# Loading and rounding down_w a second time, across the turn from the first batch to the second, in a one-core GLU kernel

## The chip, the core and the metric

The kernel runs on one core of one Trainium2 chip. The metric is the device time of one launch in microseconds (us), and the times shown are medians over runs on the chip. Engines are called PE (TensorE), DVE (VectorE), ACT (ScalarE), POOL (GpSimd) and SP (SyncE, which issues nearly all DMAs). Every engine works through its own instructions in the order in which they were written, and an instruction that has to wait for another engine or for a DMA holds up everything behind it on its engine.

## What is computed

Four batches of 1024 tokens with 512 features go through a gated block. Cut to what matters, the reference is:

```python
scale = cond @ norm_w.T + 1.0
h = x * (scale[:, None, :] * rsqrt(mean(x * x) + 1e-6))
val, gate = split(h @ up_w.T, 2)             # 2 x 2048 columns
h = val * gelu(gate)
hq = act_quant(h)                            # per token: round(h * 127 / max|h|), and back
wq = weight_quant(down_w)                    # round(down_w / mean|down_w|) cut to -1, 0, 1, and back
y = hq @ wq.T + x
```

weight_quant needs the mean of |down_w| over the whole matrix before any element can be rounded. down_w is 512 x 2048 in float32, 4 MB.

## The kernel before, in words

**Batches and slots.** The four batches run one after another, and each has 16 slots, one for every 128 columns of val and of gate. The text counts slots through the whole kernel: g = 0 to 15 is the first batch, g = 16 to 31 the second, and so on. All products of up_w are made with float16 pairs (a high and a low part).

In the first batch a slot is two calls of plain_half (L623), one for each half of 512 tokens, with 12 matmuls into a bank pg (gate), a Gelu on ACT (L629), 12 matmuls into a bank pv and a multiplication on DVE (L633). Meanwhile up_w is loaded, scaled and summed into the seven weight tiles of a Strassen product, and these sums are spilled to DRAM (s_dram, s_spill L398). The tokens of the second batch are normalized and transposed in slots 6 to 13 (class Tokens, L493).

From the second batch on a slot is one call of slot (L658) with seven products of six matmuls each, called here p0 to p6 after the number that the code gives them (L580 to L586). In the steady state PE runs p0, p4, p1 of slot g, p3 of slot g - 1, p5 of g, p2 of g - 1, p6 of g. Slot 16 has no predecessor and runs p0, p4, p5, p1, p6. p1 adds onto a bank B that ACT first fills with a copy of A after p0 (L675), p5 goes on in A after that copy, and p6 goes on in A once ACT has copied A after p5 (L668). So three short ACT copies stand between products of PE in every slot.

**Loads of the sums.** A slot's weights are loaded back from s_dram into one of two buffers SXY, in four DMAs on SP: s_load_x (L420) brings the two tiles of p0 and p1 as they are (L418, 256 KB, called part one here) and those of p4, p5 and p6 through a transposing DMA (L416, 384 KB, part two); s_load_y (L424) brings those of p2 and p3. Those of slot g + 2 are issued in slot g, each as soon as PE has read what stood in its buffer. Issuing is itself work on SP and shows in the timeline: some 0.3 to 0.6 us for a plain DMA, 1.2 us or more for a transposing one.

**down_w.** Its eight parts of 128 x 1024 (d_load, L442, 512 KB each) are loaded near the start into the half R[:, 1] of a large buffer and summed by ACT (d_sum, L446) in slots 1 to 3. Slot 4 makes the mean (d_mean, L455). From slot 5 to slot 12 ACT rounds each part where it stands (d_round, L461, an Activation of 128 x 1024) and writes its sign as float8 into a tile tn (d_put, L468, a second Activation); after every second part SP transposes tn into wd (L475), four times in all. D_ROUND (L1073) says which part in which slot. wd is read from slot 25 on, by d_sums and then by the down products.

**Order of the work.** All of it is written out by hand for the first batch (first_batch, L1093). In the later batches slot() calls back at three places x, y and z, and two lists (class Filler, L1258) hand work to DVE and to ACT there: items have a first place, a cost in us and in some cases a last place, and run in order as far as a budget goes. The list act holds the rounding of the batch before from slot 19 on. loads() (L1431) issues the s_loads at the end of a slot.

Of the kernel before, what the change touches and what calls it, by code (L numbers as in the profile page):

```python
# [9 lines left out]
F32 = mybir.dt.float32  # L10
F16 = mybir.dt.float16
BF16 = mybir.dt.bfloat16
F8 = mybir.dt.float8e4
I32 = mybir.dt.int32
AF = mybir.ActivationFunctionType
# [4 lines left out]
P = 128  # L20
EXPONENT = 0x7F800000
MAGIC = 1.5 * 2.0**23
# [29 lines left out]
def glu_quant_kernel(  # L52
# [360 lines left out]
    def s_load(g, c0, c1, turn=False):  # L413
        s, d = s_tile(g)[:, c0:c1], s_dram[g % NJ, :, c0 * 2 * HALF : c1 * 2 * HALF]
        if turn:
            SP.dma_start_transpose(s.rearrange("p c w (k f) -> p (c w k) f", k=2), d)  # L416
        else:
            SP.dma_start(out=s.rearrange("p c w f -> p (c w f)"), in_=d)  # L418

    def s_load_x(g):  # L420
        s_load(g, Y_TO, C_ALL)
        s_load(g, 0, Y_FROM, True)

    def s_load_y(g):  # L424
        s_load(g, Y_FROM + 1, Y_TO)
        s_load(g, Y_FROM, Y_FROM + 1, True)
# [8 lines left out]
    def d_part(n):  # L435
        return R[:, 1, n * HF : (n + 1) * HF]

    def d_at(n):

        return n // 4 + 2 * (n % 2), n // 2 % 2, n % 2  # L440
# [14 lines left out]
    def d_mean(part):  # L455
# [2 lines left out]
        DVE.tensor_scalar(wmean, pm, 1.0 / (D * FF), 1e-5, ALU.mult, ALU.max)  # L458
        DVE.reciprocal(wsc, wmean)

    def d_round(n):  # L461

        dn = d_part(n)
        ACT.activation(dn, dn, AF.Copy, scale=wsc, bias=MAGIC)

    tn = []

    def d_put(n):  # L468
        _, u, y = d_at(n)
        if y == 0:  # L470
            tn.append(wpool.tile([P, HF], BF16, name=f"tn_{n}", tag="v"))
        t8 = tn[-1].bitcast(F8).rearrange("p (f y) -> p f y", y=2)
        ACT.activation(t8[:, :, y], d_part(n), AF.Sign, bias=unmagic, saturate=False)
        if y:
            SP.dma_start_transpose(wd[:, n // 4, u], tn[-1])  # L475

    def w_block(name):
        k, y = W_AT[name]
# [144 lines left out]
    def plain_half(j, h, between=nothing):  # L623
        whole = j == WHOLE
        tag = ("po", 3) if whole else ("A", 2) if h or j == 1 else ("B", 1)
        pg = bank(*tag, name=f"pg_{j}_{h}")
        plain(j, 1, h, pg)
        t1 = wpool.tile([P, TOK], F32, name=f"g_{j}_{h}", tag="t1")
        ACT.activation(t1, pg, AF.Gelu, scale=gain(j, 1))  # L629
        between()  # L630
        pv = bank(*(("po", 3) if whole and not h else ("E", 2)), name=f"pv_{j}_{h}")
        plain(j, 0, h, pv)
        DVE.scalar_tensor_tensor(h_half(j, h), pv, gain(j, 0), t1, ALU.mult, ALU.mult)  # L633
# [436 lines left out]


    D_SUM = {0: (4, 5), 1: (6, 7), 2: (2, 3), 3: (0, 1)}
    D_ROUND = {5: (0, 1), 6: (2,), 7: (3,), 9: (4,), 10: (5,), 11: (6,), 12: (7,)}  # L1073
    D_MEAN = 4
    TOKENS = {6: 0, 8: 1, 10: 2, 12: 3}
    LARGEST = {
# [16 lines left out]
    def first_batch(j, sc):  # L1093

        if j + 2 <= LATE:
            w_load(j + 4)
        if j >= 4:
            next_tokens(j + 2)
        t = toks.get(j)
        odd = t is not None and j not in TOKENS  # L1100
        n = j + 2
        rows = LATE <= n < NJ
        if j + 1 < LATE:
            s_sums(j + 1)
        elif rows:
            s_sums(n)
        if j + 3 < NJ:
            w_range(j + 3)
            w_gain(j + 3)
        if j == D_MEAN:  # L1110
            part = d_total()
        plain_half(j, 0)
        for i, h in LARGEST.get(j, ()):
            for f in pair_max(0, i, h):
                f()
        if n < LATE:
            w_scale(n)
            w_rows(n)
        if j + 1 < LATE:
            s_all(j + 1)  # L1120
        if t and not odd:
            t.norm()
        for m in D_ROUND.get(j, ()):
            d_round(m)
            d_put(m)
        if t and not odd:
            t.scale(sc)
            t.sums()
        if j + 2 > LATE and j + 5 < NJ:
            w_load(j + 5)  # L1130
        if odd:
            t.high()
            t.low(DVE)
        if odd:
            t.turn()
        plain_half(j, 1)
        if j == 3:
            pd = cond_spread(dg, 1, B, "po")
            cond_undo(pd, 1, B)
            cond_rows()  # L1140
        if j == D_MEAN:
            d_mean(part)
        own = rows and j + 1 >= LATE

        def next_rows():
            if LATE <= j + 3 < NJ:
                w_scale(j + 3)
                w_rows(j + 3)

        if odd:  # L1150
            next_rows()
        if own:
            s_high(n)
            s_low(n, POOL)
        if not odd:
            next_rows()
        if own:
            s_spill(n)
        elif rows:
            s_sums(n)  # L1160
            s_all(n)
            w_load(j + 5)
        for n in D_SUM.get(j, ()):
            d_sum(n)
        if j in (NJ - 3, NJ - 1):
            s_load_x(NJ + (j - NJ + 3) // 2)
            s_load_y(NJ + (j - NJ + 3) // 2)


    def second_slot():  # L1170
# [163 lines left out]
    for b in range(1, B):  # L1334
        dve, act = Filler(), Filler()
        gains(b)
        am = am_tile(b - 1)
        dq = state[b - 1] = sm.tile([P, 2 * NA], F32, name=f"dq_{b}", tag="dq")
        last_pair = NJ // 2 - 1
        for h in range(2):  # L1340
            add_pair(
# [38 lines left out]
        for j in range(NJ):  # L1380
            g = b * NJ + j
            down = b + 1 < B and j in DOWN
            if down:
                pair, a = pairs[j], DOWN[j]
                xrs = [down_load(b - 1, h, a) for h in range(2)]
            early_sums, late_sums = D_SUM_AT.get((b, j), ((), ()))
            left = SLOT_US + PAIR_US * down - OWN_US + 0.4
            more = D_SUM_US * len(late_sums) + 0.7 * (j + 1 == min(DOWN) and b + 1 < B)
            left -= D_SUM_US * len(early_sums) + more
            mine = {p: [sum(c[e] for _, c in steps.get((j, p), ())) for e in range(2)] for p in "xyz"}  # L1390
            left -= sum(mine[p][0] for p in "xyz")
            act_left = {"x": 2.7, "y": 2.2 if down else 1.1, "z": 0}

            def run(p):
                nonlocal left
                for f, _ in steps.get((j, p), ()):
                    f()
                if p == "x":
                    cap = min(left, 3.9 - mine["x"][0] - (0 if down else mine["y"][0] + more))
                    left -= cap - dve.run((j, p), cap)  # L1400
                elif p == "z":
                    left = dve.run((j, p), left)
                if p != "z":
                    act.run((j, p), act_left[p] - mine[p][1])

            def early():
                if down:
                    pair.first([po_bank(f"po_{b}_{a}_{n}") for n in range(3)])
                    pair.sums(None, h_slots(g)[:, 0, 1])
                d_sums(early_sums)  # L1410

            def next_pair():
                if b + 1 < B and j + 1 in DOWN:
                    pairs[j + 1] = Pair(b - 1, DOWN[j + 1])
                    pairs[j + 1].sum1(h_slots(g + 1)[:, 0, 0])

            def more_sums():
                next_pair()
                d_sums(late_sums)

            mid = [nothing] * 3
            if j + 1 == min(DOWN):
                mid[0] = more_sums
            if down:
                mid = [
                    lambda: (next_pair(), pair.third(xrs, dq), d_sums(late_sums)),
                    pair.fourth,
                    lambda: (loads(), pair.fifth()),
                ]

            def loads():  # L1431
                if NJ + 2 <= g + 2 < B * NJ:
                    s_load_x(g + 2)
                if NJ + 2 <= g + 1 < B * NJ:
                    s_load_y(g + 1)


            if b + 1 == B and j in DOWN and DOWN[j] < 3:
                pairs[DOWN[j]] = Pair(b - 1, DOWN[j])
                places = old_places(DOWN[j])  # L1440
                pairs[DOWN[j]].sum1(places[0])
                pairs[DOWN[j]].sums(*places[1:])
            if j == 4:
                token_turn(b - 1, am)
            if j == 5:
                bring_dq = token_undo(b - 1, dq)
            if j == 6:
                bring_dq()
            if j == NJ - 1:
                get_ready()  # L1450
            elif b == 1 and j == 0:
                get_ready()
            slot(g, lambda: run("x"), lambda: run("y"), lambda: run("z"), early, mid)
            if not down:
                loads()
# [169 lines left out]
```

## Time and profile before

| what | value |
|---|---|
| time, median of 3 runs | 725.74 us (725.62 to 725.95) |
| span of the profiled execution | 724.0 us |
| granted TensorE clock | 1.000 |
| busy: PE, DVE, ACT, POOL | 716.5, 584.2, 397.6, 201.6 us |
| DMA moved | 117.85 MB, mean 163 GB/s |
| first batch's last matmuls (slot 15) end | about 184.2 us |

The span runs from the first to the last instruction of one profiled execution. The timed runs hold 1.7 us more, which lies around the span. A row of a timeline gives start, duration, engine, line, operation and tiles; several instructions in a row of one line are merged, with their count behind the x. In a row of windows each engine's busy time stands with its instruction count, then the granted clock (1.00 is full), the busy share of the DMA engines and the rate that they moved.

### The profile page before, as it was taken

The page shows a single profiled execution, that of the slowest core. Times are in us where ns is not written, and L with a number is a line of the kernel's source. Part 1 is how long each engine was busy: PE and PEld are TensorE (multiplying, and loading weights), DVE is VectorE, ACT ScalarE, POOL GpSimd, SP SyncE. Part 2 cuts the span into 40 slices and gives each one's busy share as a digit, 9 for nine tenths or more (in the row PEclk, how much of TensorE's full clock was granted, in tenths as well). Part 3 has the DMA queues.
Part 4 walks back from the last instruction along what each step waited for, and adds up shares of the span by engine and source line. Part 5 has one row for each costly group of instructions (what it writes and reads, how often), then busy time and mean ns, then how long its engine had stood idle before and what let it go on. Part 6 is the DMA issues. An engine that isn't in the chain of part 4 may idle for free.

```text
span 724.0 us, 10200 instructions
## 1 busy us (share of the span) xinstructions
PE 716.5 (99%) x3678; PEld 359.9 (50%) x3678; DVE 584.2 (81%) x824; ACT 397.6 (55%) x625; POOL 201.6 (28%) x207
## 2 busy tenths in 40 slices
PE   7999999999999999999999999999999999999998
PEld 3544444444444446655444445666444444445854
DVE  8977999984698899887689897687678888755896
ACT  6768868861337674554335676544433665333473
POOL 1579788882100034440000030360020000000120
PEclk9999999999999999999999999999999999999999
DMA  9579999996654564977846646766955455453253
GB/s 317 190 231 271 300 287 251 276 229 152 117 103 102 132 150 127 208 174 167 174 102 103 131 102 176 200 155 159 216 105 103 101 104 100 102 101 97 103 174 119
DMA packets 224191, 117.85 MB, mean 163 GB/s; under 512 B 186486, under 2 KB 196871, under 8 KB 224140
## 3 DMA queue, kind: packets, MB, share of 16 engines
q1 hardware_dynamic: 223850, 116.87, 66.1%
q8 instruction: 29, 0.48, 0.3%
q10 hardware_dynamic: 290, 0.33, 0.1%
q14 instruction: 22, 0.18, 0.1%
HBM read 49.50 MB, written 23.09 MB: 100 GB/s over the span
## 4 chain that ended last, share of the span: by engine, by line
PE 98%; DMA 1%; ACT 0%; SPq 0%; issue 0%; DVE 0%; ACTq 0%
PE A L586 34%; PE E L586 17%; PE pg L601 11%; PE pv L601 11%; PE po L880 9%; PE B L586 9%; PE po_end L832 4%; DMA H<-in_x_dram 1%; PE ptx L981 1%; PE pv L648 0%; PE po_B L880 0%; PE pg L648 0%; PE pw L339 0%; PE po_A L880 0%; PE po_E L880 0%; ACT R L947 0%
## 5 line engine op out<-in xcount | busy, mean ns | idle before, releaser
L586 PEld LDWEIGHTS <-SXY 128*128 128x128 f16 x2016 | 196.9, 98 | 231.3 <-issue 0.6
L586 PE MATMUL A<-R,SXY 128*128 128x512 f16 x1152 | 266.0, 379 | 0.0
L586 PE MATMUL E<-R,SXY 128*128 128x512 f16 x576 | 140.0, 379 | 0.1
L688 DVE SCALAR_TENSOR_TENSOR H<-A,sg,t 128x512 f32<-128x512 f32 x48 | 36.0, 750 | 67.9 <-PE A L586 67.7
L740 POOL PARTITION_ALL_REDUCE am<-R x8 | 14.3, 1793 | 234.0 <-DVE R L726 234.0
L804 DVE TENSOR_TENSOR H<-H,am 128x1024 f32<-128x1024 f32 x64 | 76.1, 1215 | 0.0
L601 PEld LDWEIGHTS <-SXY 128*128 128x128 f16 x486 | 47.4, 98 | 57.4 <-DVE SXY L372 0.5
L701 ACT ACTIVATE t<-t,sg 128x512 f32<-128x512 f32 x48 | 34.6, 721 | 67.8 <-DVE t L698 67.7
L586 PE MATMUL B<-R,SXY 128*128 128x512 f16 x288 | 70.0, 379 | 0.0
L724 DVE TENSOR_REDUCE gm<-H 128x512 f32<-128x1024 f32 x56 | 69.0, 1233 | 1.0
L601 PE MATMUL pg<-R,SXY 128*128 128x512 f16 x252 | 58.0, 379 | 0.0
L601 PE MATMUL pv<-R,SXY 128*128 128x512 f16 x234 | 54.4, 380 | 0.0
L685 ACT ACTIVATE t<-B,sg 128x512 f32<-128x512 f32 x48 | 33.0, 687 | 36.3 <-PE B L586 36.3
L880 PE MATMUL po<-wd,R 128*128 128x256 fp8e4 x416 | 52.5, 273 | 0.0
L490 POOL TENSOR_SCALAR ssq<-ssq 128x2 f32<-128x2 f32 x12 | 4.3, 354 | 171.2 <-ACT xt L520 122.1
L668 ACT COPY t<-A 128x512 f32<-128x512 f32 x48 | 27.9, 582 | 39.8 <-PE A L586 39.5
L880 PEld LDWEIGHTS <-R 128*128 128x128 bf16 (+1 forms) x448 | 43.8, 98 | 9.0
L680 ACT COPY v<-E 128x512 f32<-128x512 f32 x48 | 28.1, 585 | 30.9 <-PE E L586 27.7
L675 ACT COPY B<-A 128x512 f32<-128x512 f32 x48 | 27.4, 572 | 30.5 <-PE A L586 30.0
L707 DVE SCALAR_TENSOR_TENSOR H<-v,sg,t 128x512 f32<-128x512 f32 x48 | 38.5, 802 | 6.6 <-ACT t L701 6.6
L812 ACT ACTIVATE H<-H 128x1024 f32<-128x1024 f32 x38 | 39.9, 1050 | 7.1 <-DVE H L804 7.1
L726 DVE TENSOR_TENSOR R<-R,gm 128x512 f32<-128x512 f32 x56 | 42.2, 753 | 1.3
(205 smaller groups left out, 986.8 us busy)
## 6 DMA issues: line engine op xcount, KB each, us to landing
SXY<-s_dram SPq DMA_DIRECT2D x48, 256.0 KB, 3.0
s_dram<-SXY SPq DMA_DIRECT2D x18, 384.0 KB, 3.3
H<-in_L_cond_up_w_dram SPq DMA_DIRECT2D x13, 512.0 KB, 5.7
SXY<-s_dram SPq DMA_DIRECT2D x48, 128.0 KB, 3.2
xr<-in_x_dram SPq DMA_DIRECT2D x19, 256.0 KB, 3.0
out_dram<-xr SPq DMA_DIRECT2D x19, 256.0 KB, 2.6
H<-in_x_dram SPq DMA_DIRECT2D x8, 512.0 KB, 6.7
R<-in_L_cond_down_w_dram SPq DMA_DIRECT2D x8, 512.0 KB, 7.4
```

The source lines that it names most:

```text
L586: PE.matmul(o, s[:, w, k, :], tv[:, :, c, l, k, :], start=start and n == 0, stop=stop and n == len(TERMS) - 1, skip_group_check=True,)
L601: PE.matmul(ps, a[k // 2][:, w, k % 2, :], XP[:, l, k, h * TOK : (h + 1) * TOK], start=n == 0, stop=n == len(terms) - 1,)
L685: ACT.activation(cur["t1"], pb, AF.Gelu, scale=gain(g, 1))
L688: DVE.scalar_tensor_tensor(h_half(g - 1, 0), prev["A"], gain(g - 1, 0), prev["t1"], ALU.mult, ALU.mult)
L701: ACT.activation(prev["t2"], prev["t2"], AF.Gelu, scale=gain(g - 1, 1))
L707: DVE.scalar_tensor_tensor(h_half(g - 1, 1), prev["v"], gain(g - 1, 0), prev["t2"], ALU.mult, ALU.mult)
L724: DVE.tensor_reduce(gm[0], v, AX.X, ALU.max, apply_absolute_value=True)
L726: return [largest, lambda: DVE.tensor_tensor(m, m, gm[0], ALU.max)]
L804: DVE.tensor_tensor(v, v, r.to_broadcast([P, 2, TOK]), ALU.mult)
L812: ACT.activation(v, v, AF.Copy, bias=MAGIC)
L832: PE.matmul(po.rearrange("p (y c o) -> p y c o", c=2, o=P), q[:, a, h, j], wd8[:, :, j // n, j % n, :, y0:y1].rearrange("p c o y -> p y c o"),
L880: PE.matmul(po, w[:, j], m, start=start and j == 0, stop=stop and j == n - 1, skip_group_check=True,)
```

## The change

D_ROUND no longer spreads the rounding over slots 5 to 12. d_load, d_sum and the mean stay as they were. Each part is fetched again from DRAM (d_fetch) into one of three tiles that share the places xn, xt and nx of class Tokens, rounded there and its sign written (d_round, d_sign), and the pairs are transposed into wd by d_turn. Parts 0, 1 and 2 are fetched at the end of slot 13, part 3 at the end of slot 14, part 4 at the end of slot 15; parts 5, 6 and 7 go between the two halves of s_load_x in slots 16 and 17. ACT rounds part 0 in slot 14, parts 1 and 2 in slot 15, and the others in slots 16 to 19, as first items of its list. The order of the instructions on PE, DVE and POOL stays the same; ACT has the same sixteen Activations at other places, and SP eight more DMAs.

```diff
-    def s_load_x(g):
+    def s_load_x(g, between=()):
         s_load(g, Y_TO, C_ALL)
+        for f in between:
+            f()
         s_load(g, 0, Y_FROM, True)
...
+    dn = {}
+    tn = {}
+
+    def d_fetch(n):
+
+        v = wpool.tile([P, HF], F32, name=f"dn_{n}", tag=("xn", "xt", "nx")[n % 3], bufs=1)
+        c, u, _ = d_at(n)
+        SP.dma_start(out=v, in_=down_w[c * P : (c + 1) * P, u * HF : (u + 1) * HF])
+        dn[n] = v
+
     def d_round(n):
-
-        dn = d_part(n)
-        ACT.activation(dn, dn, AF.Copy, scale=wsc, bias=MAGIC)
-
-    tn = []
-
-    def d_put(n):
-        _, u, y = d_at(n)
+        ACT.activation(dn[n], dn[n], AF.Copy, scale=wsc, bias=MAGIC)
+
+    def d_sign(n):
+        y = n % 2
         if y == 0:
-            tn.append(wpool.tile([P, HF], BF16, name=f"tn_{n}", tag="v"))
-        t8 = tn[-1].bitcast(F8).rearrange("p (f y) -> p f y", y=2)
-        ACT.activation(t8[:, :, y], d_part(n), AF.Sign, bias=unmagic, saturate=False)
-        if y:
-            SP.dma_start_transpose(wd[:, n // 4, u], tn[-1])
+            tn[n // 2] = wpool.tile([P, HF], BF16, name=f"tn_{n}", tag="xr")
+        t8 = tn[n // 2].bitcast(F8).rearrange("p (f y) -> p f y", y=2)
+        ACT.activation(t8[:, :, y], dn[n], AF.Sign, bias=unmagic, saturate=False)
+
+    def d_turn(m):
+        SP.dma_start_transpose(wd[:, m // 2, m % 2], tn[m])
...
-    D_ROUND = {5: (0, 1), 6: (2,), 7: (3,), 9: (4,), 10: (5,), 11: (6,), 12: (7,)}
+    D_ROUND = {(14, 1): 0, (15, 0): 1, (15, 1): 2}
+    D_FETCH = {13: (0, 1, 2), 14: (3,), 15: (4,)}
+    D_LATE = [
+        ((0, "x"), d_round, 3), ((0, "x"), d_sign, 3),
+        ((1, "x"), d_round, 4), ((1, "x"), d_sign, 4), ((1, "y"), d_round, 5),
+        ((2, "x"), d_sign, 5), ((2, "x"), d_round, 6), ((2, "y"), d_sign, 6),
+        ((3, "x"), d_round, 7), ((3, "x"), d_sign, 7),
+    ]
+    D_MOVES = {
+        0: ((d_turn, 1), (d_fetch, 5), (d_fetch, 6)),
+        1: ((d_fetch, 7),), 2: ((d_turn, 2),), 4: ((d_turn, 3),),
+    }
...
-        for m in D_ROUND.get(j, ()):
-            d_round(m)
-            d_put(m)
+        if (j, 0) in D_ROUND:
+            d_round(D_ROUND[j, 0])
+            d_sign(D_ROUND[j, 0])
...
         plain_half(j, 1)
+        if (j, 1) in D_ROUND:
+            d_round(D_ROUND[j, 1])
+            d_sign(D_ROUND[j, 1])
...
             s_load_x(NJ + (j - NJ + 3) // 2)
             s_load_y(NJ + (j - NJ + 3) // 2)
+        if j == NJ - 1:
+            d_turn(0)
+        if j in D_FETCH:
+            for m in D_FETCH[j]:
+                d_fetch(m)
...
+        if b == 1:
+            for at, f, n in D_LATE:
+                act.add(at, 1.1, lambda now, f=f, n=n: f(n))
...
                 if NJ + 2 <= g + 2 < B * NJ:
-                    s_load_x(g + 2)
+                    moves = D_MOVES.get(j, ()) if b == 1 else ()
+                    s_load_x(
+                        g + 2, [lambda f=f, n=n: f(n) for f, n in moves]
+                    )
```

## The prediction

> **What bounds the kernel now.** I read the page first: busy times, then the chain of work that ended last.
>
> ```profile
> PE 716.5 (99%) x3678; PEld 359.9 (50%) x3678; DVE 584.2 (81%) x824; ACT 397.6 (55%) x625; POOL 201.6 (28%) x207
> PE 98%; DMA 1%; ACT 0%; SPq 0%; issue 0%; DVE 0%; ACTq 0%
> ```
>
> PE is busy 99% of the span, and the chain is PE almost throughout. An average hides stages, so the next view is the windows, cut at the head, the first batch from slot 5, the turn to the second batch, the rest, and the tail.
>
> ```profile
> 0.00:25.00 25.00, 20.92 (x106) 10.91 (x107) 20.95 (x85) 15.92 (x33) 7.55 (x13) 1.00 0.87 313
> 72.00:184.00 112.00, 112.00 (x521) 50.70 (x520) 93.81 (x119) 73.52 (x110) 80.40 (x83) 1.00 0.96 245
> 184.00:230.00 46.00, 46.00 (x215) 20.84 (x214) 36.79 (x47) 19.65 (x30) 3.59 (x2) 1.00 0.55 108
> 230.00:665.00 435.00, 434.93 (x2237) 218.34 (x2236) 344.00 (x448) 223.39 (x359) 66.84 (x71) 1.00 0.62 137
> 665.00:724.00 59.00, 55.70 (x385) 37.37 (x383) 50.56 (x70) 29.03 (x36) 7.88 (x4) 1.00 0.38 130
> ```
>
> The second number of a row is PE's busy time. From 72 to 230 us, where everything that the change touches lies, PE is busy 158.00 of 158.00 us at a granted clock of 1.00. Its idle time lies in the head (25.00 - 20.92 = 4.08 us) and the tail (3.30 us), which the change doesn't touch. So nothing can be won where work is taken away. The question is only whether the new places make PE wait.
>
> **What is removed.** ACT's work of slot 5 shows the price of a part:
>
> ```profile
> 73.25 0.68 ACT L629 ACTIVATE g<-pg,sg 128x512 f32<-128x512 f32 x1
> 73.83 1.14 ACT L464 ACTIVATE R<-R,wsc 128x1024 f32<-128x1024 f32 x1
> 75.00 1.15 ACT L473 ACTIVATE tn<-R,unmagic 128x1024 fp8e4<-128x1024 f32 x1
> 76.06 1.13 ACT L464 ACTIVATE R<-R,wsc 128x1024 f32<-128x1024 f32 x1
> 77.22 1.15 ACT L473 ACTIVATE tn<-R,unmagic 128x1024 fp8e4<-128x1024 f32 x1
> 78.28 0.67 ACT L629 ACTIVATE g<-pg,sg 128x512 f32<-128x512 f32 x1
> ```
>
> From start to start a Gelu takes 73.83 - 73.25 = 0.58 us and a pair of rounding and sign 76.06 - 73.83 = 2.23 us. Eight pairs, 17.8 us, leave slots 5 to 12, and four transposing DMAs leave SP there. PE never waited there, so this is worth 0.
>
> **What is added in slots 14 and 15.** Fetches 0, 1 and 2 stand on SP behind the loads of slot 16. SP then has nothing until part one of slot 17's load:
>
> ```profile
> 171.65 1.20 SPq L416 DMA_TRANSPOSE SXY<-s_dram  x1
> 181.60 0.33 SPq L418 DMA_DIRECT2D SXY<-s_dram  x1
> ```
>
> They are issued from 171.65 + 1.20 = 172.85 us. No row of before has such a fetch there, but a token load of the same 512 KB, on an otherwise quiet queue, is near to it:
>
> ```profile
> 239.32 0.58 SPq L512 DMA_DIRECT2D xn<-in_x_dram  x1
> 175.00:181.40 6.40, 6.40 (x31) 2.86 (x30) 2.29 (x3) 0.69 (x1) 0.00 (x0) 1.00 0.00 0
> 241.75:243.80 2.05, 2.05 (x12) 0.90 (x10) 2.05 (x3) 2.05 (x3) 0.00 (x0) 1.00 1.00 345
> ```
>
> It was issued at 239.32, and from 241.75, 2.43 us later, the DMA engines ran full (share 1.00) at 345 GB/s, by which 512 KB take 1.52 us. From 175.0 to 181.4 the DMA engines now move nothing, so the fetches have them alone. Estimate: the first lands at 172.85 + 2.43 + 1.52 = 176.8, say 177.0, the others at 178.5 and 180.0. Bounds: not before 172.85, and at the latest as slow as the eight early loads of down_w, which ran in a crowd:
>
> ```profile
> DMA to landing us min/median/max: 7.1/7.4/7.7
> ```
>
> That is 172.85 + 7.4 = 180.25. I take 177.0, because the quiet row is the nearer one. Now ACT's chain. It runs pair 0, Gelu of slot 15's first half, pair 1, Gelu of the second half, pair 2, and then the copy that slot 16 needs.
>
> ```profile
> 176.43 0.69 ACT L629 ACTIVATE g<-pg,sg 128x512 f32<-128x512 f32 x1 [4.49 <-PE pg L601]
> 181.61 0.69 ACT L629 ACTIVATE g<-pg,sg 128x512 f32<-128x512 f32 x1 [4.49 <-PE pg L601]
> 185.55 0.57 ACT L675 COPY B<-A 128x512 f32<-128x512 f32 x1 [3.25 <-PE A L586]
> 186.59 1.46 PE L586 MATMUL A<-R,SXY 128*128 128x512 f16 x6
> ```
>
> The bracket is ACT's idle time before a row: 4.49 us twice and 3.25 us, each more than a pair's 2.23. With data at 177.0 the chain is 177.0 + 2.23 = 179.23, + 0.58 = 179.81, + 2.23 = 182.04, + 0.58 = 182.62, + 2.23 = 184.85, before the copy's 185.55. The copy may start as late as 186.59 - 0.57 = 186.02 before p5 is held up. Cost 0, with 1.2 us to spare. At the late bound the chain is 180.25 + 3 x 2.23 + 2 x 0.58 = 188.10, and p5 waits 2.1 us.
>
> What queues behind these waits: on ACT the two Gelus, whose banks PE has no use for before slot 16; on SP, fetch 3 waits for the sign of part 0 (179.2), and slot 17's load behind it isn't due before 181.60.
>
> **What is added in slots 16 to 19 on ACT.** The pairs stand between the Gelu of p1's bank and the copies that release p1 of the next slot (slot 16) or p6 (slots 17 to 19).
>
> ```profile
> 189.43 0.69 ACT L685 ACTIVATE t<-B,sg 128x512 f32<-128x512 f32 x1 [0.76 <-PE B L586]
> 193.06 1.46 PE L586 MATMUL B<-R,SXY 128*128 128x512 f16 x6
> 194.62 0.69 ACT L685 ACTIVATE t<-B,sg 128x512 f32<-128x512 f32 x1 [0.77 <-PE B L586]
> 198.24 2.75 PE L586 MATMUL A<-R,SXY 128*128 128x512 f16 x12
> ```
>
> Slot 16: 189.43 + 0.58 + 2.23 + 0.57 for the copy = 192.81, and p1 starts at 193.06, 0.25 us later. Slot 17: 194.62 + 0.58 + 2.23 + 0.57 = 198.00 against 198.24. Slots 18 and 19 repeat slot 17's pattern. So these four pairs fit, with a margin of 0.24 us each. If the signal from ACT to PE eats it, each costs some 0.1 us. I count 0.1 us for the four and bound them by 0 and 0.6.
>
> **What is added on SP in slot 16, the tightest place.** Between the two parts of slot 18's load there now stand d_turn 1, which waits for the sign of part 3, and fetches 5 and 6.
>
> ```profile
> 189.37 0.33 SPq L418 DMA_DIRECT2D SXY<-s_dram  x1
> 190.66 1.40 SPq L416 DMA_TRANSPOSE SXY<-s_dram  x1
> 152.41 1.64 SPq L475 DMA_TRANSPOSE wd<-tn  x1
> 154.00:155.60 1.60, 1.60 (x9) 0.77 (x8) 1.60 (x2) 0.55 (x1) 1.54 (x2) 1.00 1.06 219
> 192.25:194.00 1.75, 1.75 (x10) 0.80 (x9) 1.00 (x2) 0.93 (x2) 0.62 (x1) 1.00 1.04 209
> 200.83 1.46 PE L586 MATMUL E<-R,SXY 128*128 128x512 f16 x6
> ```
>
> Before, part two was issued at 190.66, its data moved from 192.25 to 194.0 at 209 GB/s, and p4 of slot 18, the first to need it, starts at 200.83: about 6.8 us of slack. After, the sign of part 3 ends at 189.43 + 0.58 + 2.23 = 192.24; d_turn 1 takes SP 1.64 us (to 193.9) and two fetches 0.58 each (to 195.05), and part two is issued there, 4.4 us later than before. The data come in turn: a d_turn's began 154.00 - 152.41 = 1.6 us after its issue and moves at 219 GB/s, so its 256 KB run from 193.9 to 195.1. The fetches start 1.6 to 2.4 us after 193.9, at 195.5 to 196.3, and take 2 x 1.52 = 3.04 us, to 198.5 to 199.3. Part two's 384 KB at 209 GB/s take 1.88 us, so it lands between 200.4 and 201.2, against 200.83. It costs between 0 and 0.4 us; I take 0.2. The late bound is again 7.4 us for a fetch: 194.5 + 7.4 + 1.88 = 203.8, a wait of 3.0 us.
>
> The rounding of part 5 in slot 17 needs fetch 5, landing near 197.5, and comes after the copy at 198.0; it fits. Fetch 7 precedes part two of slot 19 on SP, whose buffer isn't read out before 199.7, and has a whole slot.
>
> **Sum.** 0 for slots 5 to 12, 0 for slots 14 and 15, 0.1 for the copies, 0.2 for p4 of slot 18: the profiled span would be 724.0 + 0.3 = 724.3, and the time, against the median 725.74 with its 1.7 us outside the span, **726.0 us**.
>
> **The rivals.** A measurement of this kernel can tell about 0.2% (1.45 us) from no change.
>
> *A, slower: the copy of slot 16 comes late.* The first fetch lands late, and ACT, waiting in order, carries it through two Gelus and three pairs into p5. It costs from a landing at 178.2 on, and decides the sign at 178.2 + 1.45 = 179.6. At the bound of 180.25 the time is 725.74 + 2.1 = 727.8. For it: the median of 7.4 us. Against it: the empty DMA window from 175.0.
>
> *B, slower: part two of slot 18 comes late.* SP waits for ACT's sign and then puts 1 MB ahead of it. It decides when part two lands after 200.83 + 1.45 = 202.3; at the bound 725.74 + 3.0 = 728.7. For it: only 0 to 0.4 us stand between the estimate and the need. Against: rates of 345 and 209 GB/s. Both together give 725.74 + 2.1 + 3.0 = 730.8.
>
> *C, PE loses its clock after a stall.* If A and B add up, PE stops for microseconds in the midst of its stream, and its granted clock may fall afterwards.
>
> ```profile
> PE pz L997 <- DVE eps L927: 1.5, 1, 1.5
> 28.00 2.59 PE pg L601 x12
> ```
>
> PE's longest wait now is 1.5 us, at the start, and the clock is 1.00 in every window; no run here shows a longer one. If one run of twelve matmuls (2.59 us) then took twice as long, the time would be 730.8 + 2.6 = 733.4.
> The Trainium skill, in "TensorE: Matmul & The Clock Gate", Part 1: The HAM clock gate, speaks for C: after an idle window of about 3.4 us the clock is halved until PE has been busy for about as long. By it a stall of 2 or 3 us alone would cost nothing more. The trace's wait of 1.5 us, with a clock of 1.00 around it, agrees but doesn't reach that window.
>
> *D, faster.* Taking 17.8 us from ACT and four DMAs from SP speeds up slots 5 to 12. Against it: 112.00 busy of 112.00. It could give the 0.07 us that PE idles later: 725.7, no change that shows.
>
> **Chances.** Forecast (0 to 1.4 us added) with D's 725.7: 0.62. A alone 0.11, B alone 0.17, both 0.06, C 0.02. Faster by over 0.2%, by something that no row shows: 0.02. So faster 0.02, same 0.62, slower 0.36. The likeliest case's own range is 725.5 to 727.2. The range for 8 in 10 must reach through A and most of B: 725.4 to 728.8.
>
> **What would show it.** Right: PE still busy 46.0 of 46.0 us between 184 and 230; fetch 0 to 2 in the window 175.0 to 181.4; ACT's copy in slot 16 still at 185.6. A shows as a wait of PE's A on ACT's copy near 187, with the roundings of slots 14 and 15 idle before a DMA. B shows as a wait of PE's E near 201 on a DMA into SXY. The steps would be wrong if the first fetch lands after 178.2, if d_turn 1 is issued later than 192.5, or if two fetches take more than 4 us together.

## The result, and the profile after

| kernel | median | runs | lowest to highest |
|---|---|---|---|
| before | 725.57 us | 17 | 724.98 to 726.16 |
| after | 727.26 us | 17 | 726.07 to 730.6 |

The ratio of after to before is 1.0028, with a 95% interval of 1.002 to 1.0036. The change makes the kernel slower by 1.7 us, and its runs spread over 4.5 us where those of before spread over 1.2 us.

The profiled execution of after has a span of 724.3 us, close to before's 724.0, and its own time of 726.07 us is the lowest of the 17. It is a lucky one, so its parts matter more than its sum. The windows first, then what PE waited for:

```profile
0.00:25.00 25.00, 22.40 (x112) 11.63 (x113) 21.44 (x88) 16.70 (x35) 7.36 (x13) 1.00 0.85 314
72.00:184.00 112.00, 112.00 (x521) 50.77 (x519) 90.67 (x116) 61.83 (x100) 79.74 (x82) 1.00 0.98 254
184.00:230.00 46.00, 45.02 (x210) 20.21 (x209) 36.44 (x47) 30.12 (x41) 3.60 (x2) 1.00 0.77 173
```

```profile
PE pz L1006 <- DVE eps L936: 1.5, 1, 1.5
PE E L595 <- DMA SXY<-s_dram: 1.0, 1, 1.0
```

Between 72 and 184 us PE is busy without a gap, as before, though ACT lost 11.7 us of work there (73.52 to 61.83). From 184 to 230 us PE lacks 0.98 us, and the second list names it: PE's E waits once, for a DMA into SXY. The head hides it in this execution. PE has done 112 matmuls by 25 us, against 106 before, and slot 16 starts at 183.05 instead of 184.00. Nothing in the head was changed: of the changed kernels below, whose heads are the same, profiles show slot 16's start anywhere from 183.0 to 184.1. So a single profile can't tell a loss of 1 us by its span; its waits can.

The place itself, in the timelines of SP and PE:

```profile
191.41 1.24 SPq L484 DMA_TRANSPOSE wd<-tn  x1
192.70 1.05 SPq L470 DMA_DIRECT2D dn<-in_L_cond_down_w_dram  x2
193.85 1.28 SPq L416 DMA_TRANSPOSE SXY<-s_dram  x1
...
201.03 1.47 PE L595 MATMUL E<-R,SXY 128*128 128x512 f16 x6 [0.98 <-DMA SXY<-s_dram]
```

The order is as written: d_turn 1, two fetches, part two of slot 18's load. That part is issued at 193.85, and p4 of slot 18 gets going at 201.03, 7.2 us later. What the DMA engines did meanwhile stands in the windows (last two columns: share and GB/s):

```profile
194.00:195.00 1.00, 1.00 (x7) 0.47 (x5) 0.04 (x1) 1.00 (x2) 0.24 (x1) 1.00 0.73 221
195.00:196.00 1.00, 1.00 (x6) 0.41 (x5) 1.00 (x2) 0.97 (x2) 0.00 (x0) 1.00 1.02 315
196.00:197.00 1.00, 1.00 (x6) 0.49 (x5) 0.97 (x3) 1.00 (x2) 0.00 (x0) 1.00 0.99 287
197.00:198.00 1.00, 1.00 (x7) 0.45 (x5) 1.00 (x3) 1.00 (x2) 0.00 (x0) 1.00 0.86 224
198.00:199.00 1.00, 1.00 (x6) 0.43 (x5) 1.00 (x2) 0.16 (x1) 0.00 (x0) 1.00 0.92 146
199.00:200.00 1.00, 1.00 (x5) 0.29 (x3) 0.80 (x3) 0.72 (x1) 0.00 (x0) 1.00 1.17 166
```

From 194 to 198 they moved 221 + 315 + 287 + 224 = 1047 KB, about the 1 MB of the two fetches (the windows don't tell them from the last bytes of d_turn 1): some 4.0 us at 262 GB/s, not 3.04. Behind them the transposing part two ran at 146 and 166 GB/s, not at 209. Part one of slot 19's load and fetch 7 are issued at 195.23 and 196.61, before part two has landed, so it stands between plain loads on both sides; which of these neighbours slows it is not shown.

### The profile page after: what moved, and what is told of

The parts are those of the page before. It is cut to its first block, busy times and chain, and to the rows that moved or that the text cites. A ratio compares the mean times of both kernels' runs of the same rounds, so it can differ in the third digit from the quotient of the medians.

```text
span 724.3 us, 10205 instructions
## 1 busy us (share of the span) xinstructions
PE 717.3 (99%) x3678; PEld 360.5 (50%) x3678; DVE 582.3 (80%) x824; ACT 397.3 (55%) x625; POOL 202.3 (28%) x207
## 4 chain that ended last, share of the span: by engine, by line
PE 95%; DVE 3%; DMA 1%; issue 0%; ACT 0%
PE A L595 32%; PE E L595 17%; PE pg L610 11%; PE pv L610 11%; PE po L889 9%; PE B L595 8%; PE po_end L841 4%; DMA SXY<-s_dram 1%; DVE gm L733 1%; PE pz L1006 1%; PE pv L657 0%; PE po_B L889 0%; DVE R L735 0%; PE pg L657 0%; DVE R L728 0%; PE po_A L889 0%
## 5 line engine op out<-in xcount | busy, mean ns | idle before, releaser
L638 ACT ACTIVATE g<-pg,sg 128x512 f32<-128x512 f32 x31 | 21.2, 683 | 40.1 <-PE pg L610 40.1
```

## The experiments

The theory after this look: part two of slot 18's load stands behind the moves of slot 16 and comes late to p4 (rival B of the prediction). Against it stand ACT's pairs holding up the copies, the 4 MB as such, and the late copy of slot 16 (rival A). All kernels are compared with the kernel before on the same chip; e1 to e8 change only the order in which DMAs are issued, or add loads that nobody uses.

**e0_same: after once more.** 

> The changed kernel as it is, for a second profile and as the reference of this group. Theory (part two of slot 18's load stands behind d_turn 1 and fetches 5 and 6 and comes late to p4 of slot 18): 727.3 us, and PE's only new wait is an E on a DMA into SXY, 1 to 3 us. Rival (the added time is spread: ACT's pairs push the copies, or the head differs): the wait for SXY is 1 us or less and the rest of the 1.7 us shows elsewhere.

Measured: 727.93 us, ratio 1.0045 (1.0028 to 1.0062). The profiled execution took 729.76 us, with a span of 728.0. What PE and its weight loads waited for there, and the windows around it (columns as above; the clock is the last but two):

```profile
PE E L595 <- DVE am L760: 2.0, 1, 2.0
...
PEld L595 <- DMA SXY<-s_dram: 2.5, 1, 2.5
```

```profile
200.00:203.00 3.00, 1.07 (x5) 0.29 (x3) 2.81 (x6) 1.29 (x2) 0.00 (x0) 1.00 1.17 171
203.00:205.00 2.00, 1.97 (x8) 0.86 (x9) 1.25 (x3) 0.46 (x1) 0.00 (x0) 0.85 1.09 364
205.00:207.00 2.00, 2.00 (x6) 0.76 (x5) 0.00 (x0) 0.12 (x1) 0.00 (x0) 0.50 0.98 243
207.00:209.00 2.00, 2.00 (x9) 0.79 (x7) 0.18 (x1) 1.85 (x3) 0.00 (x0) 0.80 0.38 117
209.00:230.00 21.00, 21.00 (x99) 9.49 (x98) 19.60 (x24) 14.59 (x19) 0.00 (x0) 1.00 0.59 116
```

The DMA engines while part two was on its way, in the same columns:

```profile
199.00:200.00 1.00, 1.00 (x6) 0.46 (x5) 1.00 (x2) 0.38 (x1) 0.00 (x0) 1.00 0.92 142
200.00:201.00 1.00, 1.00 (x5) 0.29 (x3) 0.82 (x2) 0.72 (x1) 0.00 (x0) 1.00 1.65 84
201.00:202.00 1.00, 0.07 (x1) 0.00 (x0) 0.99 (x2) 0.57 (x1) 0.00 (x0) 1.00 0.73 133
```

The wait of p4 is 1.96 us here. The first list puts it down to a DVE instruction that p4 reads nothing of; the weight loads' row names the DMA, and part two's landing, 8.1 us after its issue at 194.87, fits PE's start at 203.03. From 199 to 202 the DMA engines moved only 142, 84 and 133 GB/s, less still than in after's profile. After the wait PE's granted clock is 0.85, 0.50 and 0.80 in three windows of 2 us. That is 0.30 + 1.00 + 0.40 = 1.7 us of clock lost: half speed for 3.4 us. So 1.96 us of waiting cost 1.96 + 1.7 = 3.7 us, nearly all of the 4.0 us by which this span exceeds before's 724.0.

**e1_behind: the moves behind both parts of the load.**

```diff
         s_load(g, Y_TO, C_ALL)
-        for f in between:
-            f()
         s_load(g, 0, Y_FROM, True)
+        for f in between:
+            f()
```

> All moves put behind part two of the load instead of between its parts; same Activations at the same places, same bytes moved. Theory: no wait for SXY, 725.6 us, as before the change. Rival 1 (ACT's pairs in slots 16 to 19 hold up the copies): still 727.3 us. Rival 2 (4 MB more of traffic at this place, in whatever order, delay some load): still 727 us or a wait at another load.

Measured: 726.1 us, ratio 1.0007 (0.9998 to 1.0015). Its profile shows PE busy 46.00 of 46.00 us between 184 and 230, with the same sixteen Activations and the same 4 MB. So neither ACT's pairs nor the bytes as such cost the 1.7 us: the order on SP does. The median is still 0.6 us above before, which the interval can't tell from nothing.

**e2_turn: only d_turn 1 stays between.**

```diff
-        for f in between:
+        for f in between[:n]:          # n = 1 in slot 16
             f()
         s_load(g, 0, Y_FROM, True)
+        for f in between[n:]:
+            f()
```

> In slot 16 only d_turn 1, with its wait for the sign of part 3, stays between the two parts; fetches 5 and 6 go behind. Theory (the 1 MB ahead is what counts): part two is issued near 192.7 and lands near 196, no wait, 725.6 us. Rival (SP's wait for ACT's sign is what counts): still at least 726.5 us.

Measured: 727.76 us, ratio 1.0039 (1.0023 to 1.0055). My theory missed the time. The rival had the time right, but its mechanism isn't there: no wait for SXY shows. The timelines of ACT and PE show a third thing:

```profile
201.90 1.15 ACT L477 ACTIVATE dn<-dn,wsc 128x1024 f32<-128x1024 f32 x1 [3.90 <-DMA dn<-in_L_cond_down_w_dram]
202.95 0.70 ACT L713 ACTIVATE t<-t,sg 128x512 f32<-128x512 f32 x1
203.56 0.58 ACT L687 COPY B<-A 128x512 f32<-128x512 f32 x1
...
204.19 1.46 PE L598 MATMUL B<-R,SXY 128*128 128x512 f16 x6 [1.89 <-ACT B L687]
```

Fetch 5 now lands late. ACT's rounding of part 5 in slot 17 waits 3.90 us for it, the Gelu and the copy into B behind it are late, and PE's p1 of slot 18 waits 1.89 us. In e1, where d_turn 1 is behind as well, part two was issued at 190.08 and the fetches at 193.52; here part two waits for ACT's sign first, and the fetches follow at 195.19. So the place has two deadlines: fetch 5 for ACT and part two for PE.

**e3_turn_one: d_turn 1 and fetch 5 between, fetch 6 behind** (n = 2 in the diff above). 

> In slot 16 d_turn 1 and fetch 5 stay between the parts, fetch 6 goes behind. Theory: part two lands 2 us earlier than with two fetches (512 KB at about 256 GB/s), just before p4 needs it: 725.6 to 726.0 us. Rival (SP's wait for ACT's sign, not the bytes): 727 us as with two.

Measured: 725.53 us, ratio 1.0002 (0.9993 to 1.001). Moving one load of 512 KB by one place takes the loss away, as the theory said (725.53 us against 727.93 in the same group). The profiled execution shows rival A's wait, though, in slot 16:

```profile
179.04 1.15 ACT L477 ACTIVATE dn<-dn,wsc 128x1024 f32<-128x1024 f32 x1 [7.31 <-DMA dn<-in_L_cond_down_w_dram]
...
187.49 1.45 PE L598 MATMUL A<-R,SXY 128*128 128x512 f16 x6 [0.95 <-ACT B L687]
```

Fetch 0 came at 179.04 here and at 176.37 in after's profile. So A happens in some executions. Up to slot 16 the order is the same in after, e0_same and e1 to e4, and in their profiles fetch 0 lands 4.18, 4.26, 5.09, 4.63, 5.25 and 5.16 us after its issue. Even in e1's profile, where PE doesn't wait, the copy of slot 16 had only 0.1 us to spare.

**e4_more: one more load ahead of part two.**

```diff
-        0: ((d_turn, 1), (d_fetch, 5), (d_fetch, 6)),
+        0: ((d_turn, 1), (d_fetch, 5), (d_fetch, 6), (d_dummy, 1)),   # 512 KB, not used
```

> The changed kernel with one more load of 512 KB, whose data nobody uses, behind fetch 6 and ahead of part two of slot 18's load. Theory: the wait of p4 of slot 18 grows by what 512 KB take there, 1.5 to 2.0 us: 729 us. Rival (the wait has another cause than bytes ahead): 727.3 us, unchanged.

Measured: 729.93 us, ratio 1.0083 (1.0049 to 1.0116). That is 4.7 us above before in its group (725.24), while e0_same was 2.4 us above before in the other (725.54): 2.3 us more. Its profile has both waits:

```profile
PE E L600 <- DMA SXY<-s_dram: 2.7, 1, 2.7
PE A L600 <- ACT B L689: 1.7, 1, 1.7
```

The wait for part two, 2.66 us, is 1.7 and 0.7 us longer than in the profiles of after and e0_same. The 1.70 us are rival A's, in slot 16, before the added load is issued. So more bytes ahead of part two make p4 wait longer, but the 2.3 us are not their price alone.

**e5_late2 and e6_late6: unused loads ahead of fetch 0**, two and six of them, with the moves behind part two as in e1.

```diff
+        if j == 13:
+            d_dummy(2)                 # 6 in e6_late6
         if j in D_FETCH:
             for m in D_FETCH[j]:
                 d_fetch(m)
```

> The moves behind part two (so that p4 of slot 18 doesn't wait), and two unused loads of 512 KB ahead of fetch 0 in slot 13. Theory (rival A of the prediction as a mechanism, with its price): fetch 0 lands 2.7 us later, near 179.1, ACT's chain of 7.85 us then ends 1.9 us past what p5 of slot 16 allows: 727.5 us with a wait of PE's A on ACT. Rival (the two batches' banks absorb it): 725.6 us.

> As the one with two unused loads, but six of them, two at a time, so that fetch 0 lands near 187. Theory: PE waits 9 to 10 us in slot 16, 735.4 us, and the granted clock stays at 1.00. Rival (C of the prediction: after a wait of more than some 3.4 us PE goes on at a lower granted clock for a while): 2 to 4 us more, 737 to 739 us, with matmuls of slot 16 or 17 longer than 2.59 us for twelve and a clock below 1.00 in that window.

Measured: 731.25 us (ratio 1.0103, 1.0056 to 1.015) and 741.3 us (1.0214, 1.0184 to 1.0244; four runs from 737.58 to 742.75). ACT's chain held to the tenth, but the landing was later than I expected:

```profile
181.53 1.15 ACT L474 ACTIVATE dn<-dn,wsc 128x1024 f32<-128x1024 f32 x1 [10.18 <-DMA dn<-in_L_cond_down_w_dram]
189.35 0.58 ACT L689 COPY B<-A 128x512 f32<-128x512 f32 x1
...
185.27 1.46 PE L600 MATMUL E<-R,SXY 128*128 128x512 f16 x6 [0.40 <-DVE H L647]
189.98 2.72 PE L600 MATMUL A<-R,SXY 128*128 128x512 f16 x6 [3.26 <-ACT B L689]
```

The window in which these six matmuls start, in the columns as above:

```profile
190.00:192.00 2.00, 2.00 (x5) 0.69 (x5) 1.73 (x2) 0.44 (x1) 0.14 (x1) 0.50 1.52 227
```

In e5 the first part is rounded at 181.53, not 179.1, and 181.53 + 7.85 = 189.38 against the copy's 189.35. PE waits 0.40 + 3.26 us, and its six matmuls then show 2.72 us instead of 1.46: the clock again, 0.50 in the window from 190 to 192. So the wait alone is 3.66 us where I expected 1.9. In e6 PE waited 8.57 us and 1.99 us in slot 16, and in the window from 192 to 194 its clock was 0.50. So rival C is real as a mechanism. Its size was still too low for e6: the profiled run of 737.58 us is the shortest of the four, and the median of 741.3 lies above the 737 to 739 us expected with the clock falling.

**e7_early: fetches 0 to 2 ahead of slot 16's loads**, the moves as in after.

```diff
+        if j == 13:
+            for m in D_FETCH[j]:
+                d_fetch(m)
         if j in (NJ - 3, NJ - 1):
             s_load_x(NJ + (j - NJ + 3) // 2)
```

> The changed kernel with fetches 0, 1 and 2 ahead of slot 16's loads in slot 13 instead of behind them; the moves of slot 16 as in the changed kernel. Takes away the late landing of fetch 0 (seen as PE's A on ACT's copy, 0.95 and 1.70 us, in two profiles) and nothing else. Theory 1 (p4 of slot 18 on part two is the main loss, the late copy an extra of some executions): no wait of PE's A in slot 16, the wait of E stays, 727 us. Theory 2 (the late copy is the main loss in the timed runs): 725.8 us or less.

Measured: 727.71 us, ratio 1.0035 (1.0022 to 1.0048). The copy of slot 16 isn't late any more (ACT sat idle 0.98 us before it), and the wait of E is there with 1.81 us, the only wait of PE from 100 to 230 us:

```profile
PE E L595 <- DMA SXY<-s_dram: 1.8, 1, 1.8
```

The loss against before in the same group is 2.1 us, between the 1.7 and 2.4 us of after and e0_same. So A is the extra, and B the loss.

**e8_early_one: e7 and e3 together.** 

> Both mended: fetches 0 to 2 ahead of slot 16's loads, and fetch 6 behind part two of slot 18's load (d_turn 1 and fetch 5 ahead of it). If the two waits are all that the change costs: no new wait of PE, 725.5 us, within 0.1% of before, and all runs below 726.5 us. If ACT's pairs or the 4 MB cost something besides: 726 us or more. Not faster than before in either case, since PE had no idle time there.

Measured: 726.07 us, ratio 1.0008 (1.0000 to 1.0017), runs from 724.95 to 727.51; before in the same group had a median of 725.59 and one run of 727.37. The profile shows no new wait, and PE busy 46.00 of 46.00 us from 184 to 230. The median is within 0.1% of before, but it is 0.5 us above the 725.5 expected, just inside what I had written for "something besides", and the runs reach higher than I expected. Against a price of ACT's pairs or of the 4 MB stands e3, which has both and the same time as before. What the upper runs lost is open: no profile caught one. The mean granted clock on record for each run is a hint: the two longest, 727.33 and 727.51 us, have 0.998, the others 0.999 or 1.000, and 0.002 of 726 us is about 1.5 us. The one run of before at 727.37 us has 0.998 too, so this doesn't need the change. No version beat before, and by the windows none could, since PE had no idle time to win there.

## Why the prediction was right and where it was off

The time of 727.26 us lies in the range of 725.4 to 728.8, but not at the 726.0 forecast, and the loss of 0.28% lies beyond the 0.2% that the likeliest case stayed within. What happened is rival B, which alone had been given 0.17. The range took the result in because it was drawn to reach through A and most of B, not because the forecast was right.

- *Nothing to win in slots 5 to 12: right.* PE is busy 112.00 of 112.00 us without the rounding as with it.
- *ACT's chain: right in length, its start only in part.* From the first rounding to the copy it takes the 7.85 us of the prediction (e5). Fetch 0 was issued at 172.19 and rounded at 176.37, 4.18 us later, against 4.15 expected, but up to 5.25 us later in the other profiles. So the 1.2 us to spare were 0.85 us in after's profile, 0.1 us in e1's and nothing in e3's and e4's. The 0.1 us counted for the four copies isn't seen: in e5 PE goes on 0.05 us after ACT's copy has ended (189.35 + 0.58 = 189.93, and 189.98), less than the margin of 0.24 us. The copies that follow the pairs of slots 16 to 19 held up nothing in the profiles of after, e0_same and e7_early.
- *The step that failed is the term for part two of slot 18's load*, taken as 0.2 us between bounds of 0 and 0.4. It measured 0.98, 1.96 and 1.81 us in the profiles of after, e0_same and e7_early. Two prices under it were too low: two fetches at the 345 GB/s of a quiet row (3.04 us; some 4.0 measured), and part two at its undisturbed 209 GB/s (1.88 us; 146 to 166 GB/s measured in after, 84 to 142 in e0_same). The mechanism, the place and the deadline were right: one load of 512 KB less ahead of part two ends the loss (e3), and one more makes the wait longer (e4). Rates from a stretch with one stream were used where transposing and plain streams follow each other without a pause.
- *Rival A: happens in some executions*, 0.95 us in e3's profile and 1.70 us in e4's, from a fetch 0 that lands at 179 instead of 177. e7 shows that it isn't the main loss.
- *Rival C: given 0.02 and only after A and B together.* e0_same shows it after a wait of 1.96 us, at 1.7 us. The Trainium skill, in "TensorE: Matmul & The Clock Gate", Part 1: The HAM clock gate, has the clock halve after an idle window of about 3.4 us, and I took from it that a wait of 2 us alone would be free. The trace agrees with half the clock and with 3.4 us as the time to come back (0.50 in the middle window, 1.7 us of clock lost), but not with the idle time needed: 1.96 us was enough here, while e4's 2.66 us lost no clock. The runs of 729.8 and 730.6 us among the 17 look like it, but neither was profiled. The mean clock on record is 0.998 for the first, about 1.5 us of the span, but 0.999 for the second, which six of the other runs have as well.

## What to carry to other kernels

A DMA put between two loads on one queue costs its bytes at the rate of that crowded moment, and both what stands behind it and whoever waits for its own data have a deadline; work out both, and take the rate from a stretch as crowded as the new one will be. When PE is gapless, look for what a change adds at the place with the least slack, not for what it takes away. A short stall in a dense PE stream may cost almost twice its length through the clock, in some executions and not in others, so a wider spread of runs may be a hint of a new stall, though not a proof.

## What the runs showed of the hardware that was not expected

- A wait of 1.96 us on PE was followed by half the granted clock for 3.4 us in one execution (e0_same), one of 3.26 us after a gap of 0.40 us likewise (e5_late2), while single waits of 2.66 (e4_more), 1.89 (e2_turn) and 1.81 us (e7_early) were followed by none. In e0_same PE first ran on at a clock of 1.00 for about 1 us (the window from 203 to 204); in e5_late2 the clock fell before the wait was over (0.79 from 188 to 190).
- A transposing load whose data were through 3.3 us after its issue when it stood alone (before) landed 7.1 us (after) and 8.1 us (e0_same) after its issue behind 1 MB of plain loads.
